# Linear attention of a two-layer decoder: VectorE in program order, one range of score blocks per engine, and stage seams rearranged

## The chip, the cores and the metric

One core of one Trainium2 chip runs the whole program. The metric is device time in microseconds (us) of one execution, lower is better. The engines are TensorE (PE: matrix products; PEld: its weight loads), VectorE (DVE), ScalarE (ACT), GpSimd (POOL) and SyncE (SP), whose queue here only issues DMAs. PSUM is the memory that TensorE writes to; the other engines read it.

## The reference, cut to what matters

Two decoder layers over `x` of 16 batches, 256 positions and 256 features, all in fp32. Every sublayer is `x = x + f(layernorm(x))`:

```python
x = x + L0_attn(layernorm(x))          # causal softmax attention, 16 heads x 64, biases
x = x + L0_xattn(layernorm(x), ctx)    # attention over ctx with an additive mask, 16 x 64
x = x + L0_ffn(layernorm(x))           # RMS norm, then the 2 best of 8 experts (hidden 512)
x = x + L1_attn(layernorm(x))          # causal linear attention, 16 heads x 16
x = x + L1_xattn(layernorm(x), ctx)    # softmax attention over ctx, 16 heads x 16, biases
x = x + L1_ffn(layernorm(x))           # attention with 1 of 8 value and output experts per head
```

The linear attention, the stage that changes most, is a scan:

```python
q, k, v = elu(q) + 1, elu(k) + 1, v
S = S + k[..., :, None] * v[..., None, :]
z = z + k
out = einsum('bhde,bhd->bhe', S, q) / maximum(sum(z * q), 1e-6)
```

The last sublayer takes, per token and head, the best expert by a sigmoid gate; its gates are computed from the normalised rows alone.

## The kernel before

The program is one long launch of six stages, one for each sublayer. `x` stays in the on-chip memory for all of it: 16 tiles `xs[b]` of 128 partitions by 2x256. A batch has 256 rows, so two row tiles. The stages are numbered here 0 to 5; the change works on 3, 4 and 5 and on the start of 0.

*Order of work.* Tiles come from pools with a fixed number of buffers for each tag; an allocation waits until the buffer's last reader is done, and when a stage's pools close, the next stage's pools take over the space and wait for what used it. TensorE executes in the order of the Python program (`tc.manual_schedule(engines={PE})`). The instructions of the other engines are ordered by a scheduler that knows the dependencies and estimated costs, so an instruction of another batch can stand ahead of the one that TensorE needs next. DMAs of the SP queue are issued in the order in which they stand there, and one that must wait holds those behind it.

*Start.* `load_attention` loads four weight blocks of 1 MB in the order wq, wk, wv, wo after the first `x` tile; the biases `bq0`, `bk0`, `bv0` come after all 16 tiles of `x`. `bq0s`, the scaled bias (L107, DVE), is needed by the ACT copy of the first projected queries (L414).

*Norms.* `stats(layer, b)` is two pairs of statistics instructions on DVE (L142, L143). `rstd_one` computes 1/sqrt(var + eps) by shifts and Newton steps, a chain of about a dozen tiny instructions (L152 to L164) on DVE, or in its later part on POOL. `normed` writes the normalised rows `h`. Scratch for these comes from the current stage's pool.

*Stage 3, linear attention.* The scan is computed as masked quadratic attention: 256 positions in 2x2 blocks, of which the upper right one is empty. `SETS` lists 64 sets (b, m, o): 16 batches, two halves of the heads, two interleaved groups of four heads. `step3(s)` runs, in TensorE's order, scores of set s, weighted values of set s-2, the transposes and division of set s-3, and in turn over four steps the projections of the next half, rows and values of the next batch, and the output of an earlier one:

- `scores3`: 16 products (L1022) into two PSUM tiles of two heads each; their two diagonal blocks must be masked. DVE masks those of the first tile (L1029), ACT copies the remaining block of the first (L1030) and the whole of the second (L1031), POOL masks the second in place (L1032).
- `weighted3` (L1038, L1043) multiplies by the values, `finish3` transposes (L1054) and `normalised` divides (DVE, L930 to L932).
- `project3`: queries and keys (ps_qk); ACT writes exp and relu (L1006, L1007), DVE joins them to the feature (L1008), ACT makes two masked copies of the keys, `ks` (L1011).
- `combine(b)`: gathers the two expert outputs of the previous sublayer for every row (POOL indirect DMA, L957), adds them to `x` (DVE, L961 and L962), then statistics, `rstd` and rows `h` (L970) of batch b, all in one call, chained to the previous `combine`.
- `rows3` transposes `h` to `hT`, `values3` makes values, `out_T` (L1066) and `output3` (L1075) the output product; DVE adds it to `x` (L1079), and `rstd` for stage 4 follows, partly on POOL.

Into the same loop `fill(late, n)` puts pieces of `context4`, which prepares keys and values of stage 4 from the context: a load `c`, two products, two ACT copies into `k4` and `v4`, and stores to DRAM (`kd`, `vd`) through the SP queue. Two contexts are made before stage 3 and 14 here: 8 pieces before the loop, 3 in each step with s < 0, then 1 per step. `load_ffn` loads the last stage's expert weights `w_ve` and `w_oe` (L907, L910); a small copy on POOL (L903) holds them back until its argument is ready.

*Stage 4, cross-attention.* `prepare4` loads k and v of a batch back from DRAM (L1179, L1181), normalises rows and makes `hT` (L1192) and `q` (L1200); `keys4` makes masked, biased keys `km` (ACT, L1166), `values4` copies the values into a zero-padded tile `vpad` with a column of ones. `nms` are four tiles that are zero but for what is written later. Then scores (L1213), softmax, weighted values and transposes by steps, as in stage 3.

*Stage 5, expert attention.* For each batch, `before5` makes rows, `hT` (L1327), gate logits, the gate chain of ten DVE instructions (L1336 to L1348), transposed gates (L1353) and a store `gd`, which `pair5` reads back broadcast. Then per pair of heads: projections, scores (helper L235), softmax, and products with the expert weights. `steps5` begins with `before5(0)` alone.

Of the kernel before, what the change touches and what calls it, by code (L numbers as in the profile page):

```python
# [25 lines left out]
def decoder(ctx: ExitStack, tc: tile.TileContext, a: dict, out: bass.AP):  # L26
# [9 lines left out]
    hp = ctx.enter_context(tc.tile_pool(name="hp", bufs=2))  # L36
    wp = ctx.enter_context(tc.tile_pool(name="wp", bufs=3))
# [12 lines left out]
    def load_attention(which):  # L50
        w = weights(f"w_{which}")
        return [load_rows(w, 2048 * i, f"{which}_{n}") for i, n in enumerate(("wq", "wk", "wv", "wo"))]
# [8 lines left out]

    def load_const(name, shape, src):
        t = const.tile(shape, F32, tag=name, name=name)
        nc.sync.dma_start(out=t, in_=src)
        return t

    bq0 = load_const("bq0", [P, 8], a["a0_bq"])
    bk0 = load_const("bk0", [P, 8], a["a0_bk"])
    bv0 = load_const("bv0", [P, 8], a["a0_bv"])
# [6 lines left out]
    def ctx_rows(b, pool):  # L76

        ct = pool.tile([P, 2, S], F32, tag="c", name="c", bufs=2)
        nc.sync.dma_start(
            out=ct, in_=a["ctxT"][:, b * S : (b + 1) * S].rearrange("(c p) s -> p c s", p=P)  # L80
        )
        return ct
# [56 lines left out]
    def stats(layer, b, pool):  # L139
        st = pool.tile([P, 2, 6], F32, tag="bnst", name="bnst", bufs=2)  # L140
        for t in range(2):
            nc.vector.bn_stats(st[:, t, :], xs[b][:, t, :])  # L142
            nc.vector.bn_aggr(mvs[layer][:, 2 * b + t, :], st[:, t, :])  # L143

    def rsqrt(y, v, pool, eng):
# [4 lines left out]
        k = pool.tile([P, n], I32, tag=f"rsq_k{n}{on}", name="rsq_k", bufs=2)  # L150
        t = pool.tile([P, n], F32, tag=f"rsq_t{n}{on}", name="rsq_t", bufs=2)
# [14 lines left out]
    def rstd_one(layer, b, pool, eng=nc.vector):  # L166
# [3 lines left out]
        v = pool.tile([P, 2], F32, tag=f"rs_v{layer % 2}", name="rs_v", bufs=2)  # L170
        nc.vector.tensor_scalar(v, mvs[layer][:, 2 * b : 2 * b + 2, 1], 1e-5, None, ALU.add)
        rsqrt(rstds[layer][:, 2 * b : 2 * b + 2], v, pool, eng)
# [114 lines left out]
    def context4(b, pool, mm, wk, wv, kt, vt, queue, cpool=None):  # L287

        ct = ctx_rows(b, cpool or pool)
# [6 lines left out]
        queue.dma_start(out=kds[b], in_=k)  # L296
# [6 lines left out]
        queue.dma_start(out=vds[b], in_=v)  # L303
        yield

    def fill(gens, n):

        for _ in range(n):
            while gens and next(gens[0], 0) == 0:
                gens.pop(0)  # L310
                if len(gens) > 1:
                    next(gens[1])
# [32 lines left out]
    with ExitStack() as st:  # L345
# [19 lines left out]
        def prepare(l, b):  # L365

            if l == 0:
                stats(0, b, pool)
            rstd_one(l, b, pool)
# [129 lines left out]
        def output(l, b, t):  # L499
# [8 lines left out]
            if t == 1:  # L508
                if l == 1 and b == 0:
                    stats_tile(2)  # L510
                stats(l + 1, b, pool)

        def route(b):
# [9 lines left out]
            rsqrt(r, v, pool, nc.vector)  # L523
# [160 lines left out]
        with tc.manual_schedule(engines={mybir.EngineType.PE}):  # L684
# [5 lines left out]
            while n < len(duos) + 4 or routing:  # L690
# [6 lines left out]
                if n == len(duos) - 1:  # L697
                    w4 = []
                    for name, cols in (("x1_wqk", slice(D, 2 * D)), ("x1_wv", slice(0, D))):
# [6 lines left out]
                        context4(b, pool, mm_tile, *w4, ("qk", 2), ("v", 6), nc.scalar)  # L706
# [23 lines left out]
    with ExitStack() as st:  # L730
# [8 lines left out]
        wfqk = [load_rows(w34, 4096, "f_wq"), load_rows(w34, 5120, "f_wk")]  # L739

# [195 lines left out]

    with ExitStack() as st:
# [5 lines left out]
        last = []  # L943
# [4 lines left out]
        def combine(b):  # L948

            with ExitStack() as order:  # L950
                if last:
                    order.enter_context(tc.issue_after(last[-1]))
                for t in range(2):
                    i = 2 * b + t
                    for r in range(2):
                        y = pool.tile([P, D], F32, tag="y", name="y", bufs=4)
                        nc.gpsimd.indirect_dma_start(  # L957
                            out=y, out_offset=None, in_=yd,
                            in_offset=bass.IndirectOffsetOnAxis(ap=rows[:, i, r : r + 1], axis=0),
                        )  # L960
                        nc.vector.scalar_tensor_tensor(  # L961
                            xs[b][:, t, :], y, gates[:, i, r : r + 1], xs[b][:, t, :],  # L962
                            ALU.mult, ALU.add,
                        )
                stats(3, b, pool)
                rstd_one(3, b, pool)
                h = hs3[b] = hp.tile([P, 2, D], F32, tag="h", name="h")
                for t in range(2):
                    i = 2 * b + t
                    done = nc.vector.tensor_scalar(  # L970
                        h[:, t, :], xs[b][:, t, :], mvs[3][:, i, 0:1], rstds[3][:, i : i + 1],
                        ALU.subtract, ALU.mult,
                    )
            last.append(done.ins)
# [23 lines left out]
        def project3(b, m):  # L998
# [8 lines left out]
            nc.scalar.activation(qk, ps, AF.Relu)  # L1007
            nc.vector.scalar_tensor_tensor(qk, ex, 1.0, qk, ALU.min, ALU.add)  # L1008
# [5 lines left out]
        def scores3(b, m, o):  # L1014
            qk, ks = qks[b, m]
            at = ats[b, m, o] = pool.tile([P, 4, 3, P], F32, tag="at", name="at", bufs=3)
# [12 lines left out]
            nc.vector.tensor_tensor(at[:, 0:2, 0::2, :], sc3[0][:, :, 0::2, :], tri, ALU.mult)  # L1029
            nc.scalar.copy(at[:, 0:2, 1, :], sc3[0][:, :, 1, :])  # L1030
            nc.scalar.copy(at[:, 2:4], sc3[1])  # L1031
            nc.gpsimd.tensor_tensor(at[:, 2:4, 0::2, :], at[:, 2:4, 0::2, :], tri, ALU.mult)  # L1032
# [482 lines left out]
```

## Time and profile before

| | |
|---|---|
| median of 3 runs | 3880.46 us (3878.84 to 3884.11) |
| profiled execution | 3881.76 us |
| its span, first to last instruction | 3880.1 us |
| mean granted TensorE clock | 0.984 |
| TensorE busy | 3727.5 us, 96% of the span |
| DVE, ACT, POOL busy | 2247.5, 1617.2, 1047.2 us |
| stage 0 begins, stage 1 | 0 and about 750 us |
| stage 2 (experts of layer 0) | about 1640 to 1982 us |
| stage 3 with its entry | about 1982 to 2347 us |
| stage 4 | about 2347 to 2683 us |
| stage 5 | about 2683 to 3880 us |

The profile is of one execution. Busy time is the time in which an engine had at least one instruction running; "idle before" an instruction is put down to what released it last. The granted clock of TensorE is 1.00 at full speed and 0.50 at half: products then take twice as long and the engine still counts as busy, so a share of busy time alone doesn't show it. The terms "wait" and "releaser" below are those of the trace: A <- B means that A stood until B was done.

### The profile page before, as it was taken

To read this page: it belongs to the slowest core of one execution; us is meant where nothing else is said; L and a number is where in the kernel's file an instruction comes from. 1 tells how busy PE (TensorE), PEld (TensorE's weight loads), DVE (VectorE), ACT (ScalarE), POOL (GpSimd) and SP (SyncE) were. 2 spreads that over 40 slices of the span, in tenths; PEclk is the share of its full clock that TensorE was granted. 3 is DMA by queue.
4 is the path that set the end of the run, shared out by engine and by line. 5 is a ranking of instruction groups with operands and counts; after the bars stand their busy time and mean duration, and the time that the engine had idled before them with its cause. 6 is when DMAs were issued, how large, how long until landed. Compare 5 with 4: busy or idle time off the path is not lost.

```text
span 3880.1 us, 64795 instructions
## 1 busy us (share of the span) xinstructions
PE 3727.5 (96%) x23638; PEld 2725.1 (70%) x23638; DVE 2247.5 (58%) x6213; ACT 1617.2 (42%) x4871; POOL 1047.2 (27%) x1471
## 2 busy tenths in 40 slices
PE   8999999999999999979989898998999999999999
PEld 6777776777777777769977665665666666666666
DVE  5666667645555555532235766775655555555554
ACT  4555554555555555524435555664222122112211
POOL 3333332233343334332224653222100000000000
PEclk9999999999999999979999999998999999999999
DMA  5000000010000000032252001001222222222222
GB/s 194 1 1 1 1 1 1 1 58 15 12 17 18 12 15 17 17 85 72 72 167 100 27 14 35 29 29 23 58 60 68 61 59 66 62 60 59 68 61 49
DMA packets 88269, 171.45 MB, mean 44 GB/s; under 512 B 12448, under 2 KB 60584, under 8 KB 79760
## 3 DMA queue, kind: packets, MB, share of 16 engines
q1 hardware_dynamic: 78848, 148.51, 13.9%
q0 software_dynamic: 8528, 17.74, 1.6%
q8 instruction: 189, 3.10, 0.3%
q10 hardware_dynamic: 576, 1.05, 0.1%
q14 instruction: 128, 1.05, 0.1%
HBM read 139.57 MB, written 27.69 MB: 43 GB/s over the span
## 4 chain that ended last, share of the span: by engine, by line
PE 86%; DVE 10%; issue 1%; DMA 1%; ACT 1%; POOL 1%; SPq 0%; DVEq 0%; POOLq 0%; ACTq 0%
PE ps_qk L197 14%; PE po L1420 11%; PE ps_ve L197 11%; PE ps_v L197 6%; PE tr L266 6%; PE po L503 6%; PE sc L235 4%; PE ps_h L197 3%; PE po L885 3%; PE av L272 3%; PE sc L431 2%; PE av L488 2%; PE sc L1239 2%; PE sc L1213 2%; PE zt L1252 1%
## 5 line engine op out<-in xcount | busy, mean ns | idle before, releaser
L256 POOL TENSOR_TENSOR pr<-pr,sm 128x256 f32<-128x256 f32 (+1 forms) x384 | 309.6, 827 | 1442.1 <-DVE sm L254 1335.2
L250 ACT ACTIVATE pr<-sc,nmx 128x128 f32<-128x128 f32 (+1 forms) x768 | 315.2, 418 | 348.0 <-DVE nmx L248 312.0
L1420 PE MATMUL po<-w_oe,ut 128*128 128x256 f32 x2048 | 452.4, 379 | 0.0
L197 PE MATMUL ps_ve<-w_ve,hT 128*128 128x512 f32 x1024 | 450.8, 593 | 0.0
L1420 PEld LDWEIGHTS po<-w_oe,ut 128*128 128x128 f32 x2048 | 388.8, 190 | 52.9 <-issue 0.2
L267 ACT COPY pT<-tr 128x512 f32<-128x512 f32 (+1 forms) x256 | 136.1, 532 | 649.8 <-PE tr L266 649.8
L266 PEld LDWEIGHTS tr<-ident,pr 128*128 128x128 f32 x2176 | 270.4, 141 | 167.1 <-issue 116.4
L266 PE MATMUL tr<-ident,pr 128*128 128x128 f32 x2176 | 346.0, 275 | 13.1 <-ACT zT L497 10.3
L197 PEld LDWEIGHTS ps_ve<-w_ve,hT 128*128 128x128 f32 x1024 | 191.1, 190 | 215.3 <-issue 207.1
L446 ACT ACTIVATE pr<-sc,nmx 128x256 f32<-128x256 f32 x512 | 237.1, 471 | 251.3 <-DVE nmx L441 174.5
L452 POOL TENSOR_TENSOR pr<-pr,sm 128x512 f32<-128x512 f32 x256 | 264.1, 1053 | 283.3 <-DVE sm L450 141.6
L1392 DVE TENSOR_TENSOR tv<-ps_ve,gm 128x512 f32<-128x512 f32 x256 | 176.4, 690 | 204.6 <-PE ps_ve L197 197.6
L441 DVE CUSTOM_DVE_ANT_0 sc<-sc,mk 128x256 f32<-128x256 f32 x512 | 211.2, 444 | 112.7 <-PE sc L431 59.4
L248 DVE TENSOR_REDUCE nmx<-sc 128x2 f32<-128x256 f32 (+1 forms) x384 | 208.3, 556 | 111.0 <-ACT pr L250 106.2
L197 PE MATMUL ps_qk<-hT,w_a 128*128 128x256 f32 x1024 | 259.6, 387 | 0.0
L267 DVE COPY pT<-tr 128x384 f32<-128x384 f32 (+1 forms) x384 | 223.2, 595 | 18.6 <-PE tr L266 12.8
L197 PEld LDWEIGHTS ps_qk<-hT,w_a 128*128 128x128 f32 x1024 | 180.5, 191 | 29.6 <-issue 11.8
L197 PE MATMUL ps_qk<-hT,w 128*128 128x256 f32 x768 | 193.9, 398 | 0.0
L1219 DVE TENSOR_REDUCE nm<-sc 128x4 f32<-128x1024 f32 x128 | 150.9, 1221 | 43.3 <-PE sc L1213 43.3
L235 PE MATMUL sc<-qk 64*128 64x128 f32 (+1 forms) x1536 | 162.5, 344 | 7.8 <-ACT qk L417 5.4
L197 PEld LDWEIGHTS ps_qk<-hT,w 128*128 128x128 f32 x768 | 147.5, 203 | 19.4 <-issue 1.2
L1411 DVE TENSOR_TENSOR ut<-gr,av 128x1024 f32<-128x1024 f32 x128 | 155.3, 1214 | 5.1 <-PE av L277 5.1
(277 smaller groups left out, 6922.7 us busy)
## 6 DMA issues: line engine op xcount, KB each, us to landing
gr<-gd SPq DMA_DIRECT2D x128, 512.0 KB, 6.3
yd<-y SPq DMA_DIRECT2D x71, 128.0 KB, 1.7
c<-in_ctxT SPq DMA_DIRECT2D x32, 256.0 KB, 3.5
m_w<-in_m_w SPq DMA_DIRECT2D x16, 512.0 KB, 8.3
x<-in_x SPq DMA_DIRECT2D x16, 256.0 KB, 6.0
mk<-in_mask SPq DMA_DIRECT2D x16, 256.0 KB, 2.7
hd<-h SPq DMA_DIRECT2D x16, 256.0 KB, 2.1
w_ve<-in_f_ve SPq DMA_DIRECT2D x8, 512.0 KB, 6.5
```

Of the source, the lines that this page charges most:

```text
L197: nc.tensor.matmul(ps, lhsT=lhsT(c), rhs=rhs(c), start=(c == 0), stop=(c == 1))
L235: nc.tensor.matmul(sc[:, j, at : at + ks], lhsT=qk[rows, 0, qs], rhs=qk[rows, 1, 0:ks], start=True, stop=True,)
L248: nc.vector.tensor_reduce(nmx[:, qt, :], sc[:, :, sl], AX.X, ALU.max, negate=True)
L250: nc.scalar.activation(pr[:, j, sl], sc[:, j, sl], AF.Exp, bias=nmx[:, qt, j : j + 1], accum_out=sm[:, qt, j : j + 1],)
L256: nc.gpsimd.tensor_tensor(pr[:, :, sl], pr[:, :, sl], sm[:, qt, :].unsqueeze(2).to_broadcast([P, 2, n]), ALU.mult,)
L266: nc.tensor.transpose(tr[:, at : at + P], src, ident)
L267: copy(pT, tr[:, 0 : P * len(blocks)])
L441: nc.vector.tensor_tensor_reduce(out=sc[:, j, t, :], in0=sc[:, j, t, :], in1=mk[:, t, :], scale=-1.0, scalar=3.4e38, op0=ALU.add, op1=ALU. ...
L446: nc.scalar.activation(pr[:, j, t, :], sc[:, j, t, :], AF.Exp, bias=nmx[:, j, t : t + 1], scale=-1.0, accum_out=sm[:, j, t : t + 1],)
L452: nc.gpsimd.tensor_tensor(pr[:, j], pr[:, j], sm[:, j, :].unsqueeze(2).to_broadcast([P, 2, S]), ALU.mult)
L503: nc.tensor.matmul(po, lhsT=zTs[l, b, c][:, t * P : (t + 1) * P], rhs=wts[l][3][:, c, :], start=(c == 0), stop=(c == 7),)
L1420: nc.tensor.matmul(po[:, t, :], lhsT=ut[:, e, t * P : (t + 1) * P], rhs=woe[hp][:, e, :], start=(hp == 0 and e == 0), stop=(hp == 3 and e ...
```

## The change

Five things are done together.

1. The first attention's weights are loaded in the order wv, wq, wk, wo, and its three biases directly after them, on ACT's DMA queue.
2. Norm scratch comes from a pool `sp` of its own that lives through the whole kernel.
3. In stage 3, DVE too executes in program order, and the code is cut to write that order out: `combine` becomes `gather3`, `sums3`, `stats`, `normed3`, spread over the steps; the feature leaves `project3` for `features3`, after the scores of an odd step; the DVE part of `output3` becomes `added3`. The score tile `at` changes from [head, block] to one range of blocks for each engine: 0 to 3 DVE, 4 and 5 ACT, 6 to 11 ACT then POOL. Context tiles `c` get 3 buffers and are loaded two ahead, `k4` and `v4` get 1 each, and the stores `kd`, `vd` go through ACT's queue.
4. Stage 4 loads k and v of a batch into columns of a weight tile that stage 3 doesn't use (`kv34`), uses `ves` of stage 3 for the padded values, and its zero tiles `nms` are set before stage 3.
5. `before5(0)` runs in the last steps of stage 4, with scratch from a pool `gp` opened before that stage; `ve_stack` and `rt_stack` are closed after stage 4 instead of before.

```diff
     def load_attention(which):
         w = weights(f"w_{which}")
-        return [load_rows(w, 2048 * i, f"{which}_{n}") for i, n in enumerate(("wq", "wk", "wv", "wo"))]
+        at = {n: load_rows(w, 2048 * i, f"{which}_{n}") for i, n in enumerate(("wv", "wq", "wk", "wo"))}
+        return [at[n] for n in ("wq", "wk", "wv", "wo")]
...
         if b == 0:
             w_first = load_attention("a0")
+            bq0 = load_const("bq0", [P, 8], a["a0_bq"], nc.scalar)
+            bk0 = load_const("bk0", [P, 8], a["a0_bk"], nc.scalar)
+            bv0 = load_const("bv0", [P, 8], a["a0_bv"], nc.scalar)
-    bq0 = load_const("bq0", [P, 8], a["a0_bq"])
-    bk0 = load_const("bk0", [P, 8], a["a0_bk"])
-    bv0 = load_const("bv0", [P, 8], a["a0_bv"])
...
-    def context4(b, pool, mm, wk, wv, kt, vt, queue, cpool=None):
-        ct = ctx_rows(b, cpool or pool)
+    def context4(b, pool, mm, wk, wv, kt, vt, cpool=None):
+        ct = ctx_rows(b, cpool or pool, 3 if cpool else 2)
...
-        queue.dma_start(out=kds[b], in_=k)
+        nc.scalar.dma_start(out=kds[b], in_=k)
...
-    def fill(gens, n):
+    def fill(gens, n, ahead=1):
         for _ in range(n):
             while gens and next(gens[0], 0) == 0:
                 gens.pop(0)
-                if len(gens) > 1:
-                    next(gens[1])
+                if len(gens) > ahead:
+                    next(gens[ahead])
...
+        kv34 = [
+            [w34[:, at : at + 512].rearrange("p (c s) -> p c s", c=2) for at in (6144 + i, 6656 + i)]
+            for i in (0, 1024)
+        ]
...
+        def gather3(b):
+            for t in range(2):
+                for r in range(2):
+                    y = ys3[b, t, r] = pool.tile([P, D], F32, tag="y", name="y", bufs=4)
+                    nc.gpsimd.indirect_dma_start(
...
+        def sums3(b):
+            for r in range(2):
                 for t in range(2):
...
+                    nc.vector.scalar_tensor_tensor(
+                        xs[b][:, t, :], ys3.pop((b, t, r)), gates[:, 2 * b + t, r : r + 1],
+                        xs[b][:, t, :], ALU.mult, ALU.add,
+                    )
+
+        def normed3(b):
+            rstd_one(3, b)
...
-            nc.vector.tensor_tensor(at[:, 0:2, 0::2, :], sc3[0][:, :, 0::2, :], tri, ALU.mult)
-            nc.scalar.copy(at[:, 0:2, 1, :], sc3[0][:, :, 1, :])
-            nc.scalar.copy(at[:, 2:4], sc3[1])
-            nc.gpsimd.tensor_tensor(at[:, 2:4, 0::2, :], at[:, 2:4, 0::2, :], tri, ALU.mult)
+            nc.vector.tensor_tensor(
+                at[:, 0:4, :].rearrange("p (j a) q -> p j a q", j=2), sc3[0][:, :, 0::2, :], tri,
+                ALU.mult,
+            )
+            late2 = at[:, 6:12, :].rearrange("p (j a) q -> p j a q", j=2)
+            nc.scalar.copy(late2, sc3[1])
+            nc.scalar.copy(at[:, 4:6, :], sc3[0][:, :, 1, :])
+            nc.gpsimd.tensor_tensor(late2[:, :, 0::2, :], late2[:, :, 0::2, :], tri, ALU.mult)
...
+        def added3(b):
+            nc.vector.tensor_tensor(xs[b], xs[b], pos3.pop(b), ALU.add)
+            stats(4, b)
+            rstd_one(4, b, nc.gpsimd)
...
-            context4(b, pool, mm3, wxqk[:, :, D : 2 * D], wxv, ("k4", 2), ("v4", 2), nc.sync, vep)
+            context4(b, pool, mm3, wxqk[:, :, D : 2 * D], wxv, ("k4", 1), ("v4", 1), vep)
...
         def step3(s):
...
+            b, q = s // 4, s % 4
             if at_(s):
                 scores3(*SETS[s])
+            if q % 2 == 1 and at_(s + 1):
+                features3(*SETS[s + 1][:2])
             if at_(s - 2):
                 weighted3(*SETS[s - 2])
             if at_(s - 3):
                 finish3(*SETS[s - 3])
-            b = s // 4
-            if s % 2 == 0 and at_(s + 2):
+            if q == 0 and 0 <= b + 2 < NB:
+                gather3(b + 2)
+            if q == 1 and 0 <= b + 2 < NB:
+                sums3(b + 2)
+            if q == 2 and 0 <= b - 2 < NB:
+                added3(b - 2)
+            if q == 3 and 0 <= b + 2 < NB:
+                stats(3, b + 2)
+            if q == 0 and 0 < b + 1 < NB:
+                normed3(b + 1)
+            if q % 2 == 0 and at_(s + 2):
                 project3(*SETS[s + 2][:2])
...
-            if s % 4 == 2 and 0 <= b + 2 < NB:
-                combine(b + 2)
...
-        with tc.manual_schedule(engines={mybir.EngineType.PE}):
-            next(late[0])
-            next(late[1])
-            combine(0)
-            fill(late, 8)
-            for s in range(-3, len(SETS) + 6):
+        with tc.manual_schedule(engines={mybir.EngineType.PE, mybir.EngineType.DVE}):
+            for g in late[:3]:
+                next(g)
+            gather3(0)
+            sums3(0)
+            stats(3, 0)
+            normed3(0)
+            gather3(1)
+            fill(late, 8, 2)
+            for s in range(-3, len(SETS) + 7):
                 step3(s)
-                fill(late, 3 if s < 0 else 1)
+                fill(late, 3 if s < 0 else 1, 2)
                 if s == 10:
                     load_ffn(xs[2][0:1, 0, 0:32])
-    ve_stack.close()
-    rt_stack.close()
+    gp = ctx.enter_context(tc.tile_pool(name="gp", bufs=2))
+    hTs5, gms5, gds5 = {}, {}, {}
+    def before5(b, mm):
...
-            v4s[b] = vpad[b % 2]
+            v4s[b] = ves[b % 2]
...
-            k = pool.tile([P, 2, S], F32, tag="k4", name="k4", bufs=2)
-            nc.sync.dma_start(out=k, in_=kds[b])
-            v = pool.tile([P, 2, D], F32, tag="v4", name="v4", bufs=2)
-            nc.sync.dma_start(out=v, in_=vds[b])
-            kvs[b] = k, v
+            kvs[b] = kv34[b % 2]
+            for at, src in zip(kvs[b], (kds[b], vds[b])):
+                nc.sync.dma_start(out=at, in_=src)
...
             prepare4(0)
+            first5 = before5(0, mm4)
             for s in range(-3, len(SETS) + 5):
                 step4(s)
+                if s >= len(SETS) - 1:
+                    next(first5, None)
+
+    ve_stack.close()
+    rt_stack.close()
...
         def steps5():
-            yield [(6, before5(0))]
-            for _ in range(4):
-                yield []
             for b in range(NB):
```

## The prediction

> **What bounds the kernel now.** I read the page first (span, engine shares, chain), then the windows, then what TensorE waits for, then the timelines around those waits. Four answers follow. In windows: start and length in us, busy us of each engine, the granted TensorE clock (PEclk), DMA share. In waits: total, count, longest. In timelines: start, duration, and in brackets the idle time before and who ended it.
>
> ```profile
> span 3880.1 us, 64795 instructions
> PE 3727.5 (96%) x23638; PEld 2725.1 (70%) x23638; DVE 2247.5 (58%) x6213; ACT 1617.2 (42%) x4871; POOL 1047.2 (27%) x1471
> PE 86%; DVE 10%; issue 1%; DMA 1%; ACT 1%; POOL 1%; SPq 0%; DVEq 0%; POOLq 0%; ACTq 0%
> ```
> ```profile
> 15.00:50.00 35.00, 29.54 (x156) 21.37 (x155) 21.81 (x72) 15.82 (x61) 11.15 (x16) 0.90 0.98 337
> ...
> 1982.00:2030.00 48.00, 38.30 (x174) 31.73 (x173) 22.22 (x88) 15.49 (x26) 20.76 (x23) 0.89 0.77 251
> 2030.00:2335.00 305.00, 278.96 (x2786) 207.67 (x2786) 193.57 (x656) 170.35 (x364) 163.26 (x269) 0.95 0.16 52
> 2335.00:2360.00 25.00, 11.87 (x98) 8.10 (x100) 7.64 (x31) 6.44 (x14) 13.23 (x41) 0.89 0.19 48
> ...
> 2668.00:2712.00 44.00, 29.23 (x191) 17.67 (x190) 16.60 (x50) 14.46 (x36) 8.78 (x28) 0.77 0.22 50
> ```
> ```profile
> PE sc L1022 <- ACT at L1031: 23.9, 11, 2.4
> PE ps_k L197 <- DMA c<-in_ctxT: 9.7, 3, 8.3
> ```
> ```profile
> 2240.36 1.18 DVE L157 TENSOR_TENSOR rsq_t<-rsq_k 128x2 f32<-128x2 f32 x1
> ...
> 2243.92 0.48 DVE L961 SCALAR_TENSOR_TENSOR x<-y,gates,x 128x256 f32<-128x256 f32 x1
> 2244.32 0.69 DVE L1008 SCALAR_TENSOR_TENSOR qk<-ex,qk 128x512 f32<-128x512 f32 x1
> ```
> ```profile
> 2240.87 0.59 ACT L1007 ACTIVATE qk<-ps_qk 128x512 f32<-128x512 f32 x1
> 2245.04 0.91 ACT L1011 ACTIVATE ks<-qk,halves 128x256 f32<-128x256 f32 x2 [3.58 <-DVE qk L1008]
> 2245.86 0.77 ACT L1031 COPY at<-sc 128x768 f32<-128x768 f32 x1
> ```
> ```profile
> 2246.68 1.20 PE L1022 MATMUL sc<-qk,ks 32*128 32x256 f32 x16 [2.19 <-ACT at L1031]
> ```
> ```profile
> 2262.50:2265.90 3.40, 1.40 (x15) 0.98 (x15) 3.27 (x9) 2.44 (x6) 2.89 (x3) 0.99 0.12 34
> 2265.90:2269.30 3.40, 3.40 (x31) 2.11 (x24) 1.24 (x4) 2.12 (x5) 2.92 (x4) 0.50 0.27 82
> ```
>
> TensorE is busy 96%, so only its 153 us of idle time, and stretches at half clock, can be won. The first five windows lie where the diff works; the other rows, full or nearly full, are the stages it leaves alone. In the score stage the wait repeats once per batch: the feature instruction L1008 is ready at 2241.4 (end of ACT L1007) but runs at 2244.32, behind the norm chain of `combine` and its first sum L961. ACT waits 3.58 us for it, copies the previous scores (L1031) only then, and TensorE waits 2.19. The last two rows show the price doubled: TensorE is thin for one 3.4 us stretch and the next is granted half the clock.
>
> **The change, part by part.** All terms are against the profiled execution (3881.76 us; span 3880.1, 1.7 around it); the median shown is 1.3 lower.
>
> *1. Start.* `wv` becomes the first weight load, and the three first-stage biases go to ACT's queue instead of behind the x loads. Before, TensorE starts values at 11.65 after 2.81 us for `wv`; its projections end at 21.17; then it waits 5.38 for the bias path (`bq0s` on DVE, ACT copy L417) and scores start at 26.55, 23.3 to 30.1 being at half clock. In the new order rows are ready near 9.55 (x itself is unchanged; h costs what it did); 3.55 of values, 4.1 of ps_qk and 1.9 of values give scores at 19.1: 7.4 earlier. The clock returns about 1.8 (16 scores 2.93 against 1.58 later, and part of ps_qk). I take off 1: DVE now has norms of two batches to finish while the first softmax wants it, and `bq0s`, first on its queue, waits for a small DMA, with the first norm behind. **8 us**, bounds 5 and 10.
>
> *2. Entry of linear attention.* Stores kd/vd leave SP for ACT's queue, context tiles go from 2 buffers to 3, loaded two ahead, k4/v4 tiles from 2 to 1; `combine` is cut into `gather3`, `sums3`, `stats`, `normed3`. Before, SP stands from 1999.75 to 2008.03 at a weight load (w_ve) that waits for a POOL copy behind the gathers; the next context load sits behind it: TensorE idles 8.31 and then pays 3.75 and 3.18 instead of 1.89 for two products at half clock, 3.15 more: 11.5 in all. Afterwards nine more context loads stand ahead of w_ve, so this wait goes. New is that a single k4 is free only when its store lands: copy 0.59 plus landing 2.6 (kd) or 3.6 (vd) makes 3.3 to 4.3 us, against 3.46 of TensorE work per context (two products). Eight contexts could lose up to 6.7, cushioned by four PSUM tiles; and ACT, waiting for k4, holds back the copies and stores queued behind it. **9 us**, bounds 4 and 12.
>
> *3. Score stage.* DVE takes program order; features move to just after the scores; score blocks are laid out in one contiguous range per engine. This last I cost at 0: ACT's second copy (new L1058) still reads the PSUM tile that DVE L1052 reads and waits for it, as L1030 did; if it did save, it saves a wait that ACT has room for.
> Starts of scores run from 2089.93 (s=12) to 2323.14 (s=60): 233.2 us for 12 batches, 19.43 each. TensorE's own work per batch: scores 0.86, weighted 0.79, transposes 0.37 in each of four steps; 1.73 more for ps_qk in two, 0.44+1.74 for rows and output, 0.44+1.73 for out_T and values: 3.75+4.20+3.75+4.19 = 15.9. DVE's, by starts of successive instructions: masked copies 4x0.61, finishes 4x0.68, features 2x0.61, norm chain and rows 3.01, sums 4x0.42, added/stats/rstd 2.68, stats 1.36 = 15.1. So DVE becomes nearly as tight as TensorE.
> *A rule against it*: L157 took 1.18 above, in a loop where its sisters take 0.17, exactly while POOL's masked multiply L1032 (1.27 us) ran. The Trainium skill ("SBUF — State Buffer", section "Who interferes with whom") says that a DVE instruction with two SBUF inputs is held for the whole of a GpSimd instruction that reads SBUF, and the other way round. In program order such a hold delays everything behind it. Four L1032 per batch could by the rule each catch one: 4x1.0 → DVE 19.1, above TensorE, gain 4 us over 12 batches. By the trace one was caught per batch (11.3 us over 11): 16.1. I take the trace, for most DVE instructions then have one PSUM input; the other end is in the range.
> Going through one batch in the new order I find small waits on TensorE: rows for h behind the norm chain 0.4 to 1.0, scores for ks 0.2 to 0.6, none as long as half a clock stretch. 15.9 + 0.6 to 1.6: 16.5 to 17.5; I take 17.2. 12x(19.43-17.2) = **27 us**, bounds 12 (period 18.4) and 38 (16.3). POOL takes 4 masked multiplies at 1.27, 4 gathers at 1.0 and 12 small operations near 0.25 per batch, 12 us; its products are needed two steps (8 us) later, which covers four gathers in a row.
> *A second rule*: "TensorE: Matmul & The Clock Gate", section "HAM oscillation — how this bites in real kernels", has the clock fall only after a TensorE gap over about 3.4 us. By it, removing waits of 2.2 us wins the waits alone: 23.9, of which about 4 stay as new waits: 20. Here gaps of 2.2 in a stretch that was busy 1.40 of 3.40 already brought 0.50 in the next, in 9 places from 2108.8 to 2306.8, each worth 1.7 to 1.9 (16 in all). The trace decides.
>
> *4. Linear attention to cross-attention.* Norm scratch gets its own pool, the zero tiles are set earlier, `vpad` gives way to `ves`, k and v of a batch load into an old weight tile. Before, the last output product ends at 2347.0; transposes wait 0.78, ps_q 0.72, and scores start at 2359.14 after 8.82, because k loads only at 2353.58, once the old pools are released and a POOL chain is done. Afterwards the loads need no new pool; km's space is free when output ends; six km copies, hT and two q copies on ACT bring scores at about +4.9 instead of +12.1. 7.2, and about 2 of the 10 us at half clock. The two loads wait on SP for the vd stores, which the old fence awaited too. **9 us**, bounds 6 and 10.
>
> *5. Into the last stage.* The first gates (`before5(0)`) run in the last steps of cross-attention. Before, TensorE waits 0.72, 0.72, 7.94, 0.74 and 1.66 and works mostly at half clock from the last transposes (2682.8) to the first expert product (2709.97): 27.2 us. With ps_qk at about 2683.5, three ps_qk groups and their scores at full clock and a wait of 2.9 for the single score tile, the first expert product comes near 2695.5: 14.5 less, minus about 1.5 for the gate products put among the last steps, where TensorE has short waits anyway (2.8 in six). **13 us**, bounds 9 and 15.
>
> Unchanged stages: 0. Sum 8+9+27+9+13 = 66: 3815.8 for the profiled execution, 3814.5 as a median.
>
> **Rivals.**
> *DVE becomes the bound.* Holds as in the rule above, period 19.1: term 3 is 4 instead of 27, total 43: 3837. For it: 15.1 of work against 15.9 of TensorE. Against: one hold per batch seen.
> *Stores choke the entry.* k4/v4 single, cycle 4.3: term 2 falls to 2: 3821. For it: vd landings up to 7.5 while big loads run. Against: those loads now come later.
> *Slower: gathers head the line.* In program order a late gather stops DVE and all behind it, where the scheduler put other work first. Gathers landed in 2.7 to 6.9 us. If `sums3` waited 6.9 each batch, the period is 24.1 and 12 batches lose 56, more than the 39 of the other parts: 3898. It decides from 19.43+39/12 = 22.7 us. Against: gathers are issued a step (4 us) and more ahead, and 6.9 occurred only while big weights were loading.
> *The change doesn't separate the engines*: that is in my forecast at 0.
>
> **How the numbers follow.** Forecast (period 16.5 to 18): 0.78; DVE bound 0.12; choked entry 0.06; gathers 0.04. Distances of the bounds from the terms, added as squares, are 17 down and 12 up: 49 to 78 us, 3802 to 3832. The range takes in the DVE-bound case and a little more on the fast side: 3798 to 3842. A measurement here tells about 0.2% (7.8 us) from no change. Slower by more: 0.03; same: 0.02; faster: 0.95.
>
> **What would show it.** The wait of L1022 on ACT (23.9) nearly gone, starts of scores 17.2 apart per batch, clock 1.00 through the score stage; first scores near 19; no TensorE wait of 8 us on a context load; scores of cross-attention 5 us after the last output; ps_gT no longer waiting 7.9. DVE over 95% busy in the score stage, with L157-like holds several times a batch, or `sums3` waiting on a DMA, would prove me wrong.

## The result, and the profile after

The changed kernel takes 3846.53 us (median of 4 runs, 3844.84 to 3849.59) against 3879.65 us before (4 runs on the same chips). The ratio is 0.9913, 95% interval 0.9896 to 0.9931: 33 us faster, half of the 66 that were forecast, and outside the forecast range (3798 to 3842). The profiled execution took 3849.59 us, its span is 3847.9.

The page of the changed kernel: its head, the engines, and the chain by engine.

```profile
span 3847.9 us, 64735 instructions
PE 3716.0 (97%) x23638; PEld 2715.6 (71%) x23638; DVE 2276.2 (59%) x6213; ACT 1618.1 (42%) x4871; POOL 1041.1 (27%) x1467
PE 87%; DVE 11%; issue 1%; ACT 1%; POOL 0%; DMA 0%; DVEq 0%; POOLq 0%; ACTq 0%
```

TensorE's busy time fell by 11 us, and its time at half clock from about 126 to about 75 us. Where the time went is read by following one event of each stage through both traces (start in us, and how much earlier it comes):

| event | before | after | earlier by | forecast for the part |
|---|---|---|---|---|
| first scores of stage 0 | 26.55 | 19.68 | 6.9 | |
| first value product of stage 1 | 749.75 | 744.75 | 5.0 | start: 8 |
| last product of stage 2 ends | 1979.89 | 1976.22 | 3.7 | 0 |
| scores of set 0, stage 3 | 2027.51 | 2013.25 | 14.3 | entry: 9, came 10.6 |
| scores of set 12 | 2089.93 | 2075.11 | 14.8 | |
| scores of set 60 | 2323.14 | 2315.01 | 8.1 | score stage: 27, came -6.7 |
| last output product of stage 3 ends | 2347.03 | 2337.58 | 9.5 | |
| scores of stage 4 | 2359.13 | 2341.78 | 17.4 | 9, came 7.9 |
| first expert product of stage 5 | 2709.97 | 2677.68 | 32.3 | 13, came 14.0 from the last transposes |
| end of the span | 3880.1 | 3847.9 | 32.2 | |

The four seams gave 37.5 of the 39 that were forecast for them, and the score stage, the largest term, lost 6.7 instead of winning 27. The windows of the changed kernel around the same places show it (columns as before):

```profile
15.00:45.00 30.00, 26.81 (x152) 19.01 (x151) 22.54 (x70) 15.90 (x61) 11.08 (x15) 1.00 1.02 358
1976.00:2014.00 38.00, 34.76 (x174) 29.86 (x172) 9.11 (x31) 14.68 (x25) 12.63 (x16) 1.00 0.67 210
2014.00:2325.00 311.00, 276.30 (x2786) 202.82 (x2782) 230.51 (x703) 172.46 (x366) 166.07 (x274) 0.98 0.20 64
2325.00:2350.00 25.00, 18.42 (x170) 12.06 (x168) 17.50 (x50) 10.30 (x21) 14.78 (x43) 1.00 0.13 38
2650.00:2680.00 30.00, 24.16 (x182) 15.07 (x175) 16.99 (x50) 14.44 (x36) 9.12 (x29) 0.94 0.34 73
```

In the seams (all rows but the third) the clock is back at 1.00, in the last at 0.94. The third row, 311 us with 276 busy, is the one to read. TensorE's waits in the entry and the score stage (1960 to 2330):

```profile
PE ps_hT L997 <- DVE h L988: 27.3, 14, 2.8
PE sc L1045 <- ACT ks L1032: 6.0, 10, 1.1
```

The old wait, scores on an ACT copy behind the features, is gone, as forecast. In its place stands the transpose of the rows `h`, about 2 us in every batch. Of the four steps of a batch (from the scores of a set to the next set's; medians), the first and third take 3.75 us, as TensorE's own work forecast; the second takes 6.72 instead of 4.20, the fourth 5.65 instead of 4.19. In the second, what is late is the norm chain on DVE, here in the timeline of the changed kernel:

```profile
2157.82 0.42 DVE L173 TENSOR_SCALAR rs_v<-mv 128x2 f32<-128x2 f32 x1
2158.28 1.20 DVE L154 TENSOR_SCALAR rsq_k<-rs_v 128x2 int32<-128x2 int32 x1
...
2160.89 1.21 DVE L159 TENSOR_TENSOR rsq_t<-rsq_k 128x2 f32<-128x2 f32 x1
...
2162.53 0.73 DVE L988 TENSOR_SCALAR h<-x,mv,rstd 128x256 f32<-128x256 f32 x2
```
```profile
2156.96 2.50 POOL L1059 TENSOR_TENSOR at<-at,tri 128x512 f32<-128x512 f32 x2
2160.82 1.26 POOL L1059 TENSOR_TENSOR at<-at,tri 128x512 f32<-128x512 f32 x1 [1.37 <-ACT at L1057]
```
```profile
2160.45 0.44 PE L1083 MATMUL tr_o<-ident,os 128*128 128x128 f32 x2
2163.08 0.78 PE L997 MATMUL ps_hT<-ident,h 128*128 128x128 f32 x4 [2.19 <-DVE h L988]
```

Three instructions that take 0.17 elsewhere take 0.42, 1.20 and 1.21, each ending when a multiply on POOL ends: 2.3 us of holds in one chain, from 2157.82 to the end of `h`. Without them `h` would have been there at about 2160.9, when TensorE came for it.

A second loss shows in the fourth step and has no line of its own. At the end of the third, DVE stands 2.71 us for a transpose that had ended at 2167.61:

```profile
2166.59 0.68 DVE L1052 TENSOR_TENSOR at<-sc,tri 128x512 f32<-128x512 f32 x1
2169.98 0.17 DVE L937 TENSOR_SCALAR dn<-tr_o 128x8 f32<-128x8 f32 x1 [2.71 <-PE ps_qk L199]
```
```profile
2167.17 0.44 PE L1083 MATMUL tr_o<-ident,os 128*128 128x128 f32 x2
2167.45 1.89 PE L199 MATMUL ps_qk<-hT,w 128*128 128x256 f32 x8
```
```profile
2165.76 0.99 POOL L968 DMA_INDIRECT y<-yd,rows  x1 [3.67 <-DVE x L978]
2167.05 0.96 POOL L968 DMA_INDIRECT y<-yd,rows  x1 [0.30 <-issue]
2168.32 0.95 POOL L968 DMA_INDIRECT y<-yd,rows  x1 [0.30 <-issue]
2169.58 0.96 POOL L968 DMA_INDIRECT y<-yd,rows  x1 [0.31 <-issue]
```

The releaser that the profile names (ps_qk) isn't what L937 needs. The trace also holds the time of each signal, the semaphore update by which TensorE tells other engines that a product is done. The signal of `tr_o` came 2.35 us after its end, and those of the products around it 0.6 to 2.1 us late, while the four gathers of a batch ran in a row on POOL. From scores 12 to 60 the kernel before has no signal of TensorE later than 0.3 us (median 0.02); the changed kernel has 52 of 252. (The profile models the ends of products, so it can't tell a late signal from a late product.) DVE's waits for the transposes in that stretch, before and after:

```profile
DVE dn L930 <- PE tr_o L1054: 14.1, 12, 1.7
```
```profile
DVE dn L937 <- PE ps_qk L199: 27.4, 10, 2.9
```

Because DVE is now in program order, everything behind L937 (added3, statistics, the next masked copy, the features) is late with it, and the step from values to scores takes 5.65 us instead of 4.19. The two losses are the theories A (holds) and B (late results) of the experiments; theory C is that DVE simply has too much work.

### The profile page after: what moved, and what is told of

Read it like the earlier page. It is cut to its first block, busy times and chain, and to the rows that moved or that the text cites. A ratio compares the mean times of both kernels' runs of the same rounds, so it can differ in the third digit from the quotient of the medians.

```text
span 3847.9 us, 64735 instructions
## 1 busy us (share of the span) xinstructions
PE 3716.0 (97%) x23638; PEld 2715.6 (71%) x23638; DVE 2276.2 (59%) x6213; ACT 1618.1 (42%) x4871; POOL 1041.1 (27%) x1467
## 4 chain that ended last, share of the span: by engine, by line
PE 87%; DVE 11%; issue 1%; ACT 1%; POOL 0%; DMA 0%; DVEq 0%; POOLq 0%; ACTq 0%
PE ps_qk L199 14%; PE po L1468 11%; PE ps_ve L199 11%; PE ps_v L199 7%; PE tr L268 6%; PE po L505 6%; PE sc L237 4%; PE ps_h L199 3%; PE po L892 3%; PE av L274 3%; PE sc L433 2%; PE av L490 2%; PE sc L1315 2%; PE sc L1289 2%; PE zt L1328 1%; DVE sc L443 1%
## 5 line engine op out<-in xcount | busy, mean ns | idle before, releaser
L269 DVE COPY pT<-tr 128x384 f32<-128x384 f32 (+1 forms) x384 | 223.1, 594 | 19.1 <-PE tr L268 13.1
L199 PE MATMUL ps_qk<-hT,w 128*128 128x256 f32 x768 | 183.3, 382 | 0.7 <-DVE zn L939 0.7
L868 DVE COPY wt<-m_w 128x1024 f32 x71 | 49.3, 694 | 188.0 <-PE ps_h L199 186.2
```

The source lines that it names most:

```text
L199: nc.tensor.matmul(ps, lhsT=lhsT(c), rhs=rhs(c), start=(c == 0), stop=(c == 1))
L269: copy(pT, tr[:, 0 : P * len(blocks)])
```

## The experiments

Each ran beside the kernel before on its chip, and is compared by its ratio to it. "Period" is a twelfth of the time from scores 12 to scores 60: 19.43 before, 19.99 changed. "Holds" are the excess of DVE instructions in that stretch over the duration that the same instruction has where nothing holds it: 12.0 us before, 26.2 changed. A signal is called late from 0.3 us on.

### Holds: without POOL's masked multiply

```diff
-            nc.gpsimd.tensor_tensor(late2[:, :, 0::2, :], late2[:, :, 0::2, :], tri, ALU.mult)
```

> The changed kernel without POOL's masked multiply of the second score tile (its diagonal blocks stay unmasked). Theory A (holds): POOL's multiply holds three small instructions of the norm chain for 1.0 us each, in the stretch for which TensorE's rows wait. Then the chain falls from 5.4 to about 3.0 us, the rows' wait of 27.3 us vanishes, the score stage's period falls from 19.99 to 17.2 or 17.5, and the time to about 3814. Theory B (DVE starts its chain late, because results of TensorE reach it late once per batch, while the gathers run): rows still wait about 2 us, period 19 or more, 3835 to 3846. Theory C (DVE simply has too much work): period about 19.99 less 2.3 of holds.

3814.08 us, ratio 0.983 (0.9814 to 0.9846). Holds are 0, the period is 17.36. The waits of TensorE from scores 12 to 60, and then of DVE:

```profile
PE ot L1071 <- issue: 4.2, 10, 0.5
PE sc L1045 <- ACT ks L1032: 3.5, 9, 0.4
```
```profile
DVE dn L937 <- PE ps_qk L199: 24.4, 9, 2.7
```

The wait for rows is gone, as theory A had it, with its period and time; late signals are still there (60), so theory B is alive.

### Late results: without gathers on POOL

```diff
-                    nc.gpsimd.indirect_dma_start(
-                        out=y, out_offset=None, in_=yd,
...
+                    at = P * (2 * b + t)
+                    nc.sync.dma_start(out=y, in_=yd[at : at + P, :])
```

> The changed kernel with the 64 gathers of the score stage replaced by plain loads of rows in order on SP's queue, so other rows are added to x. Theory A: holds come from the multiply, so the three held instructions and the rows' wait stay, period 19 to 20, 3835 to 3847. Theory B: without gathers on POOL the results of TensorE reach DVE and ACT at once, the idle 2.7 us of DVE per batch goes, the step from values to scores falls from 5.65 to about 4.2, period 18.5, 3829.

3816.55 us, ratio 0.9833 (0.9817 to 0.985). No signal is late, the step is 4.19 as theory B said, the period 17.69, better than its 18.5. Holds of 19.2 us stay, and with them a wait for rows of 17.4 (before the edit 24.5 in this stretch). Each theory explains a part.

### Neither

```diff
-                    nc.gpsimd.indirect_dma_start(
...
+                    at = P * (2 * b + t)
+                    nc.sync.dma_start(out=y, in_=yd[at : at + P, :])
...
-            nc.gpsimd.tensor_tensor(late2[:, :, 0::2, :], late2[:, :, 0::2, :], tri, ALU.mult)
```

> The changed kernel with POOL's masked multiply left out (diagonal blocks of the second score tile unmasked) and with the gathers of the score stage replaced by plain loads of rows in order on SP's queue (other rows are added). If holds and late results are separate and together make up the whole loss of the score stage, the period falls from 19.99 to TensorE's 15.9, and the time to about 3797 to 3800. If they are one loss seen twice, the period is about 17.4, like the better of the two alone, and the time 3812 to 3815.

3795.75 us, ratio 0.9776 (0.976 to 0.9793); period 16.09. Windows from scores 12 to 60, of the changed kernel and then of this one:

```profile
2075.11:2315.01 239.90, 205.58 (x2113) 148.51 (x2113) 187.10 (x572) 128.91 (x276) 131.36 (x230) 0.97 0.08 23
```
```profile
2069.71:2262.78 193.07, 192.96 (x2114) 142.83 (x2113) 161.28 (x572) 129.75 (x276) 31.98 (x140) 1.00 0.10 29
```

TensorE is busy 192.96 of 193.07 us. The two causes are the whole loss: 3.9 us per batch together. DVE has the same 572 instructions as in the changed kernel, 161 us without the holds, so theory C is out. One by one the edits gave 2.6 and 2.3; the sum of these is 1.0 larger, of which about 0.6 is the four stretches at half clock (1.7 each), which either edit alone removes; the rest was not resolved.

### The norm chain one step earlier

```diff
                 stats(3, b + 2)
-            if q == 0 and 0 < b + 1 < NB:
-                normed3(b + 1)
+                normed3(b + 2)
```

> The changed kernel with the norm chain of a batch written one step earlier (directly behind its statistics), same instructions. Theory A: the holds may stay, but the rows are ready a step before TensorE needs them; the wait of 27.3 us goes, unless the chain now delays the masked copy behind it: period 17.5 to 18, 3818 to 3825. Theory C: DVE's work is unchanged, so the period stays near 20 and the wait moves to the scores: 3844 to 3850.

3876.21 us, ratio 0.9985: 28 us worse than the changed kernel, period 22.1. Both forecasts missed, though theory A's "unless" names what happened. TensorE's waits:

```profile
PE sc L1045 <- ACT at L1058: 33.5, 12, 3.0
PE sc L1045 <- ACT ks L1032: 7.8, 10, 1.2
```

The rows no longer wait, but the chain now stands in front of the masked copy L1052 of the next step. ACT's L1058 waits for that copy, and the next scores for L1058, since the PSUM score tiles hold one set. Nothing long may stand ahead of L1052.

### DVE left to the scheduler

```diff
-        with tc.manual_schedule(engines={mybir.EngineType.PE, mybir.EngineType.DVE}):
+        with tc.manual_schedule(engines={mybir.EngineType.PE}):
```

> The changed kernel with DVE in stage 3 ordered by the scheduler again; everything else as changed. If program order is what costs the score stage, the period is at or below that of the kernel before, 19.4 or less, and the time 3840 or lower. If program order helps and something else of the change (gathers in one row, single buffers, the new score layout) costs, the period rises above 20 and the time above 3850.

3886.02 us, ratio 1.0008: the gain is gone. The steady period is better, 18.8, but scores start at 2029.41 and the first twelve sets take 97.5 us instead of 61.9. The split code without a written order lets the scheduler put all 64 gathers into one nearly unbroken row from 1980 to 2080; signals are up to 6.2 us late in it. Each side of the expectation holds by half: the period falls, the time rises. The written order is needed at the entry; what it costs in the steady part this run can't say, for no gathers or sums are left there. The next run has them.

### The old order with the new queues

```diff
-            if q == 0 and 0 <= b + 2 < NB:
-                gather3(b + 2)
...
+            if s % 4 == 2 and 0 <= b + 2 < NB:
+                combine(b + 2)
...
-        with tc.manual_schedule(engines={mybir.EngineType.PE, mybir.EngineType.DVE}):
+        with tc.manual_schedule(engines={mybir.EngineType.PE}):
```

> The changed kernel with the order of the score stage undone (combine in one call, features and output sums where they were, DVE ordered by the scheduler); the seams, the stores on ACT's queue, three context tiles, single k4 and v4, the norm pool and the new score layout stay. If program order cost the 7 us that the steady score stage lost and the queues alone mended the entry, about 3840. If program order is also what keeps the entry short, 3850 to 3865.

3851.58 us, ratio 0.9918 (0.9901 to 0.9934), not to be told from the changed kernel's 0.9913. It is the second side of the expectation. Period 19.30 and no late signal, so the written order loses 0.7 per batch (8 us); scores start 4.5 us later and the first twelve sets take 69.6, 7.7 more. The written order pays at the entry what it loses afterwards: the 33 us are those of the seams and queues.

### The score layout

```diff
-            at = ats[b, m, o] = pool.tile([P, 12, P], F32, tag="at", name="at", bufs=3)
+            at = ats[b, m, o] = pool.tile([P, 4, 3, P], F32, tag="at", name="at", bufs=3)
...
```

> The changed kernel with the score tile laid out as before (by head, the ranges of the engines interleaved); order and gathers as changed. Theory L: TensorE's results reach DVE and ACT 2 us late while gathers run only since the layout changed (the kernel before ran three gathers in a row with no such lag): then the lag vanishes, the step from values to scores falls from 5.65 to about 4.2 and the time to 3818 to 3830. Theory G: four gathers in a row are enough: lag and time stay, 3843 to 3852, or a little more if the layout did help.

The copies, masks and products address the tile as before the change again. 3848.43 us, ratio 0.9913: equal. The layout is worth 0, as forecast, and late signals don't come from it.

### Gathers one by one; Newton steps on POOL; both

```diff
-            if q == 0 and 0 <= b + 2 < NB:
-                gather3(b + 2)
...
+            nb, i = (b + 2, 3) if q == 0 else (b + 3, q - 1)
+            if 1 < nb < NB:
+                gather3(nb, [i])
```

> The changed kernel with the four gathers of a batch spread, one behind the masked multiply of each step, instead of four in a row. Theory G (a row of gathers holds back TensorE's results): lag gone, DVE no longer stands 2.7 us per batch, step from values to scores about 4.2, rows' wait 27 down to about 17 as in the run without gathers; 3817 to 3822. Theory of the gather itself (each costs its share wherever it stands): the lag is spread over four steps, 3835 to 3850.

Each gather is also put behind the masked multiply before it. 3849.97 us, ratio 0.9915. Signals are under 0.8 late and the fourth step is back at 4.19, but the expected gain didn't come: gathers now stand between POOL's multiplies, the norm chain meets the end of a gather and the multiplies behind it, and fewer holds (24 for 34) last longer. They rise to 33.0 us and the wait for rows to 31.3, with ten stretches at half clock.

```profile
PE ps_hT L1000 <- DVE h L991: 31.3, 13, 2.9
```

```diff
         def normed3(b):
-            rstd_one(3, b)
...
                 stats(3, b + 2)
+                rstd_one(3, b + 2, nc.gpsimd)
...
```

> The changed kernel with the Newton steps of the stage-3 norm put on POOL (one step earlier), so that POOL's own multiply can no longer hold them and DVE has 9 small instructions less per batch. Theory A (holds): rows' wait of 27.3 us goes to 0 to 5, the lag of the gathers stays; about 3817 to 3825. If POOL becomes the bound (12 us of work plus 3 per batch) or its chain comes too late for the rows, 3840 or more.

3861.95 us, ratio 0.9945: worse, in the way that the second half of the expectation named. POOL's chain comes too late:

```profile
DVE h L987 <- POOL rstd L166: 38.8, 12, 3.4
```

> Both: gathers spread and the Newton steps on POOL. If the two causes are separate, their gains add: period near 16 to 16.5, score stage 42 to 48 us shorter than in the changed kernel, about 3800. If they are one cause, 3815 to 3820, no better than the better of the two.

The edits of both. 3844.27 us, ratio 0.9901. Signals are at most 0.62 late, but `h` still waits 43.4 us for POOL's chain; period 19.75 instead of 16 to 16.5. The gains did not add, because this cure of the holds brings a wait of its own; it doesn't speak against two separate causes.

### DVE's steps evened out, gathers one by one and in pairs

```diff
         def normed3(b):
-            rstd_one(3, b)
...
+
+        def rest3(b):
             stats(4, b)
             rstd_one(4, b, nc.gpsimd)
...
+            if q == 2 and 0 <= b + 2 < NB:
+                stats(3, b + 2)
             if q == 3 and 0 <= b + 2 < NB:
-                stats(3, b + 2)
+                rstd_one(3, b + 2)
             if q == 0 and 0 < b + 1 < NB:
                 normed3(b + 1)
+            if q == 0 and 0 <= b - 3 < NB:
+                rest3(b - 3)
...
```

> The changed kernel with the gathers spread, one behind each step's masked multiply, and DVE's work per step evened out: statistics of batch b+2 in the third step, its Newton steps in the fourth, the rows h in the first of the next batch, the second norm's statistics moved there too. Rows are then ready a step early, so holds (2 to 2.8 us per batch) no longer lie on TensorE's path. If the path is what counts, period 16.5 to 17.5, 3804 to 3818. If DVE's sum counts (15.1 of work and 2.8 of holds per batch), period 18 or more, 3822 or more, with the wait on the scores instead.

`normed3` now makes only the rows `h`, and `rest3` is the second half of `added3`; the gathers are the single ones of the run above. 3814.14 us, ratio 0.9824 (0.9808 to 0.9841); period 17.33: 36 us less than the same single gathers in the changed kernel's order (3849.97). The pairs differ in the gathers:

```diff
-            nb, i = (b + 2, 3) if q == 0 else (b + 3, q - 1)
-            if 1 < nb < NB:
-                gather3(nb, [i])
+            if q in (1, 3) and 1 < b + 3 < NB:
+                gather3(b + 3, [q - 1, q])
```

> As the balanced kernel, with the gathers in two pairs per batch. Tells what makes TensorE's results late: if only three or four gathers in a row do, no result is late and the time equals the balanced kernel's within 4 us; if two do, results come 1 to 2 us late twice per batch, and it is 5 to 20 us slower.

3812.38 us, ratio 0.9818 (0.9802 to 0.9835), equal to the singles. No signal is over 0.3 late in either. These compute all that the changed kernel does and beat it by about 35 us. Windows and waits of the pairs from scores 12 to 60:

```profile
2073.07:2280.03 206.96, 191.18 (x2113) 142.53 (x2113) 189.07 (x568) 129.70 (x276) 142.69 (x234) 1.00 0.10 28
```
```profile
PE sc L1047 <- ACT ks L1034: 15.8, 10, 1.6
```

DVE is as busy as in the changed kernel (189 us against 187), which is 91% of the stretch instead of 78%, and its holds are larger (30.2 us, 29.1 of them on the features), yet the stretch is 33 us shorter. The sum of DVE's work doesn't set the period; what stands in front of what TensorE needs does. The remaining 1.3 us per batch is a held feature.

### Four and three gathers in a row, in the evened order

```diff
-            if q in (1, 3) and 1 < b + 3 < NB:
-                gather3(b + 3, [q - 1, q])
+            if q == 1 and 1 < b + 3 < NB:
+                gather3(b + 3)
```

> The balanced kernel with all four gathers of a batch in one row behind the sums, as in the changed kernel. If four in a row are what makes TensorE's results late, they are late by about 2 us once per batch again, DVE stands 2 to 3 us per batch, and the time is 5 to 20 us above the pairs' 3812. If the lateness belongs to the changed kernel's order, none is late and the time stays within 4 us of 3812.

3838.76 us, ratio 0.9882; signals up to 3.3 us late once per batch, period 19.35. The loss is a little more than the 5 to 20 us expected.

```diff
-            if q == 1 and 1 < b + 3 < NB:
-                gather3(b + 3)
+            if q in (1, 3) and 1 < b + 3 < NB:
+                gather3(b + 3, range(3) if q == 1 else [3])
```

> The same with three gathers in a row and the fourth two steps later. The kernel before ran three in a row and no result was late there: if the length of the row decides, none is late here, and the time is within 4 us of 3812. If the place in the step or the spacing decides (before: 1.36 us apart; changed: 1.26), results are late by 1 to 2 us, and the time lies between the pairs and the four in a row.

3828.69 us, ratio 0.9855; up to 2.6 late, period 18.62. Against the pairs, a row of four costs about 25 us and a row of three about 15, with nothing changed but the places of the gathers. The waits of DVE in the run with four show the sign again, a transposed tile named as released by a later product:

```profile
DVE dn L937 <- PE ps_v L199: 16.8, 8, 2.1
```

The length of the row isn't all: the kernel before and the one with the old order also ran three in a row and had no late signal. There the gathers came 1.36 us apart, here 1.25 to 1.29. Whether the spacing is the reason, and by which way a gather on POOL delays a signal of TensorE, stays open.

## Why the prediction was wrong, by its own steps

*Start: 8, came 5.0.* The first scores came at 19.68 (forecast 19.1) and no stretch at half clock followed. The step that was too small is the DVE and ACT backlog, taken as 1: TensorE has three new waits there, 1.7, 1.1 and 0.5, 3.3 in all. Another 1.3 was lost in stages 1 and 2, forecast at 0: stage 2's two stretches at half clock became 23.9 us each instead of 20.5.

*Entry: 9, came 10.6.* Right in size, in part by luck. The wait of 8.3 for a context load is gone, and single k4 and v4 did not choke it. But from the end of stage 2 to the first scores it was 47.6 us before, 41.8 in the run with the old order and 37.0 in the changed kernel: the queues gave 5.8, and 4.8 came with the written order, for which the sum had no term.

*Score stage: 27, came -6.7.* This is the failure. The features did leave the norm's shadow and the wait of 23.9 went. Two steps failed.
First "I take the trace": one hold of 1.0 per batch, and with it "rows for h behind the norm chain 0.4 to 1.0". In program order the holds became 2.2 per batch (26.2 us over 12), all on the norm chain that the rows wait for, and the rows' wait 2.0 (24.5 us). Without the multiply both were 0 and the period 17.36; that this is near the forecast 17.2 is chance, for the late results are still in it. The rule of the Trainium skill ("SBUF — State Buffer", section "Who interferes with whom") had been weighed at 19.1 us per batch and set aside, and 19.1 is nearer to 19.99 than 17.2. But it is not its sum that came true: DVE was 78% busy, not full, and the evened order has more holds and is faster. Count of holds in the old order says nothing on a new one; the place has to be read from the new order against POOL's.
Second, "DVE's, by starts of successive instructions" had no term for results that come late. The move of four gathers into one row was costed by POOL's time alone ("covers four gathers in a row") and found free. It cost 2.3 us per batch (the run without gathers).
The clock, third term of the stage, behaved as argued, but "none as long as half a clock stretch" failed with the first step: with waits of 2 us, four stretches at half clock remained, with the waits gone none did.

*Linear to cross-attention: 9, came 7.9. Into the last stage: 13, came 14.0.* Right in mechanism and size. Scores of stage 4 come 4.2 us after the last output (forecast 4.9). The two places in the changed kernel:

```profile
2341.78 1.15 PE L1289 MATMUL sc<-km,q 32*128 32x256 f32 x16 [0.81 <-ACT q L1276]
...
2673.02 0.93 PE L237 MATMUL sc<-qk 64*128 64x128 f32 x8 [2.08 <-ACT pr L252]
...
2677.68 2.88 PE L199 MATMUL ps_ve<-w_ve,hT 128*128 128x512 f32 x6
```

The 8.8 us ahead of the first are 0.8; ps_gT's 7.9 have become a 2.1 at the single score tile (forecast 2.9).

*Layout: 0.* Right, by its own run.

*Rivals.* "DVE becomes the bound" (3837) was nearest, with the wrong reason: place, not sum. "Gathers head the line" named the right culprit and the wrong path: `sums3` never waited for a landing. Of the signs against the forecast, holds several times a batch were there; DVE over 95% busy was not.

## What to carry to other kernels

When an engine is put in program order, sum its work for each step, not for the whole period, and ask of every instruction what another engine needs from behind it: the same work with the same single gathers, evened over the steps, was 36 us faster. An order also fixes which instructions of two engines run against each other, so holds that met a chain once per batch (12.0 us in all) can meet it two or three times (26.2), now where TensorE waits for it. A helper's burst of gathers isn't costed by its own engine alone: look whether other engines stand for results that were already there.

## What the runs showed of the hardware that was not expected

- From scores 12 to 60, TensorE's completions reached DVE and ACT up to 3.3 us late while three or four gathers (about 0.96 us each, about 1.26 apart) ran in a row on POOL, and at the entry up to 6.2 late in a row of dozens; with pairs, none was over 0.3 late. In the profile it looks like a wait for a later product of TensorE.
- POOL's multiply also holds DVE instructions with one input in SBUF: `rsq_k<-rs_v` took 1.20 instead of 0.17, and `rs_v<-mv` 1.97 in the run with single gathers, where it met the end of a gather and a multiply. In the changed kernel without the multiply all holds were 0.
- TensorE at 192.96 us busy of 193.07 stayed at clock 1.00; stretches at half clock in this stage came only after waits of about 2 us or more. What decides seems to be the busy share of one 3.41 us stretch, the unit in which the clock changes in these traces: the stretch ahead of each fall was busy at most 0.49 in the kernel before and in the changed one (at most 0.59 in any run), the others at least 0.52. The pairs' wait of 1.6 us left 0.52 and cost no clock.
